# Reordering the prologue of a convolution-and-attention kernel on one core

## The chip, the core and the metric

The kernel runs on one core of one Trainium2 chip. The metric is the device time of one execution in microseconds; a comparison uses the median of several runs. The core has five engines that run side by side and meet through semaphores: TensorE (PE in the profile; its weight loads are PEld), VectorE (DVE), ScalarE (ACT), GpSimd (POOL) and SyncE (SP), whose queue issues every DMA of this kernel. Each engine takes its instructions strictly in the order in which the program gives them.

## The reference

Eight images of 128 channels and 36x36 pixels go through two layers. What matters of them:

```python
# layer 0, on the group-normalised image; residual added outside
x = conv1x1(gn(x), w_x) + b_x
q = conv3x3(x, w_qx, 'SAME');  k = conv3x3(x, w_kx, 'VALID');  v = conv3x3(x, w_vx, 'VALID')
a_x = softmax(q^T k) v
h = tanh(conv1x1(concat([x, a_x], 1), w_h) + b_h)
out = conv1x1(h, w_o) + b_o

# layer 1, on the 1296 tokens of 128 channels of each image
t = tanh(q[:, :, None, :] + k[:, None, :, :])          # additive attention
attn = softmax(einsum('bijd,d->bij', t, w) + bw)
t = t_in + attn @ ln(t_in)
t = t + moe(ln(t))       # 64 experts, each takes its 8 best tokens of an image
```

The input also has a context image `c0` (one value for each channel). It enters `h` only through a constant vector: since a softmax sums to one, the attention over a constant context is its value convolution. The kernel computes that vector once.

## The kernel before

All arrays are float32. The kernel has a prologue for the first image, a long score loop over all images, and an end for the experts.

**The score loop.** The additive attention is written with products of features: for the queries and the keys of a token the kernel keeps exponentials of eight blocks of 128 projected features, and a score is a sum of quotients of matrix products. `units` lists (image, chunk of 432 queries, tile of 128 keys), 8 x 3 x 11 in all, and `slots` cuts a unit into 12 slots (2 for the short last key tile). In each slot `numerators` and, three slots ahead (`LAG`), `denominators` issue small matrix products (L875). ScalarE takes a logarithm and an exponential to invert the denominators (L898, L901), and VectorE and GpSimd multiply and sum (`terms`, L923 to L938). The key features of a tile (`kf`, 512 KB) come from HBM: `keys` computes them (L645, L649), stores them to `kd` (L660), and `prefetch` (L858) loads them two units ahead.

**Work for the next image** is written as generators: `normal` (group normalisation, the 1x1 convolution and the windows for the 3x3 ones), `conv_keys`, `layer0`, `tokens`, `keys`. In the loop four lanes take one piece of a generator at a time between slots, by fixed rules; for the first image the prologue runs the generators through one after another (`drain`). The order of instructions on each engine is thus fixed when the program is built.

**The prologue**, in the order in which it is issued:

- L165 to L179: loads of x of the first image, `w_x`, `b_x` and the small constants; GpSimd fills constants meanwhile (L181 to L213).
- L217 to L227: the context vector: `w_vc` is loaded (576 KB), nine small products and one more make `vc` and then `hb`, the bias of layer 0's tanh.
- L1010: x of the second image is loaded.
- `normal(0)` (L318): it begins with `load_taps` for the keys (L323). The 3x3 convolutions use a scheme with four turned taps in place of three, so `load_taps` loads the raw taps (L304 to L306), turns them on VectorE (L308 to L311) and stores the result in HBM (L313), from where later images load it (L300). Then the statistics of x (L327, L330), two products with the group average `gavg`, the reciprocal root on GpSimd (L239), the scaled weights `wxn` on GpSimd (L350), the 1x1 convolution (L360) and its windows on VectorE (L362 to L375).
- `signs` (L495): GpSimd builds a matrix of signs, 128x1024, with a memset and 22 selects (L505); the features of layer 1 need it.
- `conv_keys(0)`, then `features` (L512): two loads, two transpositions, four products with the sign matrix (L528), and a few small products (L538, L550) that make the constants `a_q`, `a_k`, `cs_s`, `fb_s`, `eb_s` of the loop.
- `layer0(0)` (L390): `load_taps` for values and queries, the value convolution in three groups of rows with four parts each (L403), its product with `w_h` (`pvw`, L411), then for each chunk of 432 pixels the query convolution, the attention, and at last the tanh and the output product.
- `tokens(0)`, the keys of three tiles, three query blocks, `prefetch` of two units, and the denominators of the first three slots.

`big` is a pool of eight buffers for images, taps and the like; `chunks` holds smaller ones. `TAKE`, `step` and `matmuls` are what a generator yields to say what it wants next; `bmm` is a matmul that is counted for the loop's balance, and the profile puts it on L258 (transpositions: L262).

Of the kernel before, what the change touches and what calls it, by code (L numbers as in the profile page):

```python
# [2 lines left out]

# [66 lines left out]
def kernel(  # L70
# [55 lines left out]
    with ExitStack() as loop, ExitStack() as score:  # L126
# [37 lines left out]

        load_x(0)  # L165
        wx_s = loaded(w_x, "w_x")
        bx_s = loaded(b_x, "b_x")
        wh_s = loaded(w_h, "w_h")
# [4 lines left out]
        gw_s = loaded(gate_w, "gate_w")  # L173
        gb_s = loaded(gate_b, "gate_b")
# [4 lines left out]
        nc.sync.dma_start(bw_s, bw.to_broadcast([128, 1]))  # L179
        neg_half = const.tile([128, NT], F32, tag="neg_half", name="neg_half")  # L180
# [33 lines left out]

        wvc_s = big_tile("wvc_s")[:, : 9 * C]  # L217
        nc.sync.dma_start(wvc_s, w_vc.rearrange("i t o -> i (t o)"))
        pv = aux("pv")
        for t in range(9):  # L220
            mm(pv[:, :1], wvc_s[:, t * C : (t + 1) * C], c0_s, start=(t == 0), stop=(t == 8))
        vc = small.tile([C, 1], F32, tag="vc", name="vc")
        nc.vector.tensor_copy(vc, pv[:, :1])
        ph = aux("ph")
        mm(ph[:, :1], wh_s[:, 2, :], vc, start=True, stop=True)
        hb = const.tile([C, 1], F32, tag="hb", name="hb")
        nc.vector.tensor_add(hb, ph[:, :1], bh_s)  # L227
# [65 lines left out]
        turned_taps = {}  # L293

        def load_taps(w, name):

            t = big_tile(name)[:, : 12 * C]
            h = t.rearrange("p (y j c) -> p y j c", y=3, j=4)
            if name in turned_taps:
                nc.sync.dma_start(t, turned_taps[name])  # L300
                return h
            g = w.rearrange("i (y x) o -> i y x o", x=3)
            g1 = chunk_tile("g1")[:, : 3 * C].rearrange("p (y c) -> p y c", y=3)
            nc.sync.dma_start(h[:, :, 0, :], g[:, :, 0, :])  # L304
            nc.sync.dma_start(h[:, :, 3, :], g[:, :, 2, :])
            nc.sync.dma_start(g1, g[:, :, 1, :])  # L306
            half = chunk_tile("half")[:, : 3 * C].rearrange("p (y c) -> p y c", y=3)
            nc.vector.tensor_add(half, h[:, :, 0, :], h[:, :, 3, :])  # L308
            nc.vector.tensor_scalar(half, half, 0.5, None, ALU.mult)
            nc.vector.scalar_tensor_tensor(h[:, :, 1, :], g1, 0.5, half, ALU.mult, ALU.add)  # L310
            nc.vector.scalar_tensor_tensor(h[:, :, 2, :], g1, -0.5, half, ALU.mult, ALU.add)  # L311
            turned_taps[name] = dram.tile([C, 12 * C], F32, tag=name, name=f"{name}_d")
            nc.sync.dma_start(turned_taps[name], t)  # L313
            return h
# [3 lines left out]
        def normal(b):  # L318
# [4 lines left out]
            taps["k"] = load_taps(w_k, "wk_t")  # L323
# [20 lines left out]
            ve = plus_eps(pv[:, :1], 1e-5, [C, 1])  # L344
            yield step(2)
# [37 lines left out]
        def conv_keys(b):  # L383
            k = convolved["k"] = big_tile("k0")
            for r0, nr in KROWS:
                yield from conv_turns(
                    taps["k"], (r0, nr), 1, grid(k[:, r0 * WV : (r0 + nr) * WV], WV), True
                )

        def layer0(b):  # L390
# [5 lines left out]
            wv_t = load_taps(w_v, "wv_t")  # L396
            v = big_tile("v0")
            wq_t = load_taps(w_q, "wq_t")
# [112 lines left out]

        def features(sign):  # L512
# [4 lines left out]
            feat = []  # L517
            for name, wt in (("a_q", wq1), ("a_k", wk1)):
                wt_s = chunk_tile("w_in")[:, :C]
                nc.sync.dma_start(wt_s, wt)  # L520
# [501 lines left out]
        for u in range(2):  # L1022
            prefetch(u)
        for p in range(LAG):
            denominators(p)
# [221 lines left out]
```

## Time and profile before

| | us |
|---|---|
| median of 3 runs | 6183.36 (6181.84 to 6194.64) |
| profiled execution, its own time | 6189.61 |
| its span in the profile | 6187.9 |
| TensorE, ScalarE, VectorE, GpSimd busy | 5946.4, 5275.0, 4799.7, 4584.2 |

Milestones of the profiled execution, from the timeline:

| start, us | what |
|---|---|
| 0.81 | x is issued |
| 12.30 | first product of the context |
| 19.17 | statistics of x |
| 23.09 | `ve`, the variance with epsilon |
| 27.00 | first row of the window buffer (`xpad`) |
| 36.05 to 45.15 | results of the key convolution are added up |
| 25.59 to 50.35 | GpSimd's selects for the signs |
| 60.62 | first product of the value convolution |
| 70.39 | it goes on after a wait |
| 80.22 | first `pvw` |
| 152.18 | output product of layer 0 |
| 172.17 | first keys |
| 183.58 | first denominators of the loop |

The page gives the busy time of each engine, the span in slices, the chain that ended last and the costliest groups of instructions. The timeline lists instructions in order of time with start and duration; the waits list says who waited for whom, the time in total, the count and the longest. In the table of stretches each row has the stretch, its length, the busy time of TensorE, its weight loads, VectorE, ScalarE and GpSimd with counts, then the clock that TensorE was granted (1.00 is full), the busy share of the DMA engines and the GB/s they moved. A matmul in float32 shows as two records.

### The profile page before, as it was taken

How to read it: one execution, taken by the hardware profiler on the slowest of the kernel's cores; microseconds unless marked ns; L12 is line 12 of the kernel's file. 1: busy time of each engine (PE TensorE's matmuls, PEld its weight loads, DVE VectorE, ACT ScalarE, POOL GpSimd, SP SyncE). 2: the span in 40 equal slices, each digit the busy share in tenths (PEclk: the TensorE clock that was granted, in tenths of full speed). 3: DMA queues.
4: the chain of work that ended last, by engine and by line, in shares of the span. 5: the costliest groups of instructions: out<-in, count | busy, mean ns of one | idle time of the engine just before them, and what ended most of it. 6: DMA issues, size and time to landing. Idle time of an engine off the chain costs nothing.

```text
span 6187.9 us, 93159 instructions
## 1 busy us (share of the span) xinstructions
PE 5946.4 (96%) x33576; PEld 2834.5 (46%) x33576; DVE 4799.7 (78%) x9525; ACT 5275.0 (85%) x5371; POOL 4584.2 (74%) x2794
## 2 busy tenths in 40 slices
PE   7999999999999999999999999999999999999996
PEld 5454444544544445444445444454444444544443
DVE  3687778877788787877887777887778878788872
ACT  1798998988989888889988899898998988999980
POOL 3677877777778777778777786877777777787870
PEclk9999999999999999999999999999999999999997
DMA  1210011000110002100111001110011000100017
GB/s 43 70 36 22 21 68 38 33 26 28 67 39 24 26 30 69 37 24 23 50 48 38 22 24 63 41 36 22 21 65 41 31 25 28 63 31 28 25 55 276
DMA packets 150383, 271.40 MB, mean 44 GB/s; under 512 B 45408, under 2 KB 74976, under 8 KB 149920
## 3 DMA queue, kind: packets, MB, share of 16 engines
q1 hardware_dynamic: 149920, 265.44, 12.8%
q8 instruction: 265, 4.34, 0.3%
q14 instruction: 198, 1.62, 0.1%
HBM read 200.94 MB, written 64.19 MB: 43 GB/s over the span
## 4 chain that ended last, share of the span: by engine, by line
PE 65%; DVE 11%; POOL 8%; ACT 8%; issue 8%; DMA 1%; SPq 0%; POOLq 0%; DVEq 0%; ACTq 0%
PE n L875 30%; PE d L875 10%; PE pa L258 7%; ACT lq L898 5%; PE pc L258 5%; DVE n L923 4%; POOL accp L938 4%; DVE rp L929 3%; PE s L258 3%; PE pk L258 3%; DVE accd L925 2%; POOL qf L673 1%; POOL accp L936 1%; PE d L880 1%; PE pq L258 1%
## 5 line engine op out<-in xcount | busy, mean ns | idle before, releaser
L938 POOL TENSOR_TENSOR accp<-accp,rp 128x864 f32<-128x864 f32 x1440 | 2915.1, 2024 | 996.5 <-DVE rp L929 943.5
L875 PE MATMUL n<-qf,kf 32*128 32x432 f32 (+1 forms) x11520 | 3283.6, 574 | 58.9 <-DVE accd L925 19.1
L898 ACT ACTIVATE lq<-d 128x864 f32<-128x864 f32 x2928 | 2517.6, 879 | 555.8 <-PE d L875 498.0
L875 PE MATMUL d<-qf,kf 32*128 32x432 f32 (+1 forms) x11520 | 2907.7, 563 | 46.4 <-ACT lq L898 40.5
L929 DVE TENSOR_TENSOR rp<-n,lq 128x432 f32<-128x432 f32 x3912 | 2160.8, 600 | 557.9 <-PE d L875 398.8
L901 ACT ACTIVATE lq<-lq 128x1728 f32<-128x1728 f32 (+1 forms) x1464 | 2398.2, 1638 | 46.3
L875 PEld LDWEIGHTS n<-qf,kf 32*128 32x128 f32 (+1 forms) x11520 | 1185.9, 185 | 1588.2 <-DVE rp L929 469.1
L875 PEld LDWEIGHTS d<-qf,kf 32*128 32x128 f32 (+1 forms) x11520 | 1046.9, 186 | 449.8 <-issue 241.7
L923 DVE TENSOR_TENSOR n<-n,lq 128x432 f32<-128x432 f32 x1440 | 812.0, 608 | 251.8 <-PE n L875 195.2
L925 DVE TENSOR_TENSOR accd<-n,accd 128x432 f32<-128x432 f32 x1440 | 868.1, 603 | 24.7
L936 POOL TENSOR_TENSOR accp<-rp 128x864 f32<-128x864 f32 x240 | 485.2, 2022 | 244.8 <-DVE rp L929 244.7
L673 POOL TENSOR_SCALAR qf<-qf,cs_s 128x432 f32<-128x432 f32 x192 | 260.7, 1364 | 47.0 <-ACT qf L672 47.0
L258 PEld LDWEIGHTS pa<-xh,e 128*108 128x108 f32 x1920 | 222.1, 174 | 142.9 <-DVE rp L929 63.3
L947 POOL TENSOR_TENSOR accd<-accp,accd 128x432 f32<-128x432 f32 x240 | 265.3, 1106 | 23.3 <-DVE accd L925 3.0
L258 PE MATMUL pa<-xh,e 128*108 128x129 f32 x1920 | 261.3, 283 | 19.9 <-DVE accd L925 13.9
L945 POOL TENSOR_TENSOR accp<-accp 128x432 f32<-128x432 f32 x240 | 264.7, 1103 | 15.8
L258 PE MATMUL s<-q,k 128*116 128x432 f32 x480 | 230.3, 568 | 4.2 <-DVE accd L925 2.7
L444 ACT ACTIVATE e<-s 116x432 f32<-116x432 f32 x240 | 124.8, 520 | 118.7 <-PE s L258 118.4
L258 PEld LDWEIGHTS pk<-xT,a_k 128*128 128x128 f32 x1408 | 171.6, 193 | 105.9 <-DVE n L923 31.8
L435 POOL TENSOR_TENSOR tot<-tot,e 116x432 f32<-116x432 f32 x192 | 212.1, 1105 | 7.3 <-ACT e L444 4.5
L918 DVE TENSOR_TENSOR accd<-n,lq 128x432 f32<-128x432 f32 x240 | 145.1, 604 | 86.7 <-PE n L875 49.7
L258 PE MATMUL pa<-e,vw 116*128 116x432 f32 x480 | 204.6, 549 | 0.0
(208 smaller groups left out, 3870.2 us busy)
## 6 DMA issues: line engine op xcount, KB each, us to landing
kf<-kd SPq DMA_DIRECT2D x240, 512.0 KB
kd<-ks SPq DMA_DIRECT2D x160, 256.0 KB
w<-in_weight_dram SPq DMA_DIRECT2D x32, 1024.0 KB
wk_t<-wk_t_d SPq DMA_DIRECT2D x7, 768.0 KB
wv_t<-wv_t_d SPq DMA_DIRECT2D x7, 768.0 KB
wq_t<-wq_t_d SPq DMA_DIRECT2D x7, 768.0 KB
x<-in_x_dram SPq DMA_DIRECT2D x8, 648.0 KB
t<-tokd SPq DMA_DIRECT2D x96, 54.0 KB
```

The lines of the kernel that those rows point to most:

```text
L258: mm(out, lhsT, rhs, **kw)
L673: nc.gpsimd.tensor_scalar(qf[:, 1, :], qf[:, 0, :], cs_s[:, q : q + 1], None, ALU.mult)
L875: mm(outs[h][:, :CH], kf[rows[h], q, :], qf_of[b, c, q][rows[h], part, :], start=True, stop=True)
L898: nc.scalar.activation(lq[:, o : o + n, :], d[:, :n, :CH], AF.Ln)
L901: nc.scalar.activation(some, some, AF.Exp, scale=-1.0)
L923: mult(ns[h], ns[h], lq[:, o + h, :])
L925: nc.vector.tensor_add(live["d"], ns[h], live["d"])
L929: mult(rp[:, h, :], n, lq[:, o + h, :])
L936: nc.gpsimd.tensor_add(live["p"], live["r"], rp)
L938: nc.gpsimd.tensor_add(live["p"], live["p"], rp)
L945: nc.gpsimd.tensor_add(s[:, 0, :], s[:, 0, :], s[:, 1, :])
L947: nc.gpsimd.tensor_add(d, s[:, 0, :], d)
```

## The change

- The raw taps of keys, values and queries are loaded at the start, right behind x, `w_x` and `b_x`, together with the two inputs of `features`; the other constants follow. x of the second image is loaded when its `normal` begins.
- Turning the taps is a function of its own, `turn_taps`, with an engine as argument and five operations instead of four. For the keys it runs on VectorE, in `normal(0)` behind `ve`; for values and queries on GpSimd, between `normal(0)` and `signs`.
- The context vector and `features` become generators, chained. From the tenth piece of `layer0(0)` on, one of their pieces is issued after each of its pieces; what is left follows behind.
- Only one tile of keys is made before the first query blocks and denominators. Its exponentials go to a `kf` buffer directly and are stored from there; no `prefetch` of unit 0 is made. The next two tiles and the `prefetch` of unit 1 follow behind the denominators.

```diff
+        def load_raw_taps(w, name):
+            h = big_tile(name)[:, : 12 * C].rearrange("p (y j c) -> p y j c", y=3, j=4)
+            g = w.rearrange("i (y x) o -> i y x o", x=3)
+            g1 = chunk_tile("g1")[:, : 3 * C].rearrange("p (y c) -> p y c", y=3)
+            nc.sync.dma_start(h[:, :, 0, :], g[:, :, 0, :])
+            nc.sync.dma_start(h[:, :, 3, :], g[:, :, 2, :])
+            nc.sync.dma_start(g1, g[:, :, 1, :])
+            raw_taps[name] = (h, g1)
+
         load_x(0)
         wx_s = loaded(w_x, "w_x")
         bx_s = loaded(b_x, "b_x")
+        load_raw_taps(w_k, "wk_t")
+        w_in = [loaded(w, "w_in", chunks, "chunk") for w in (wq1, wk1)]
+        load_raw_taps(w_v, "wv_t")
+        load_raw_taps(w_q, "wq_t")
         wh_s = loaded(w_h, "w_h")
...
-        wvc_s = big_tile("wvc_s")[:, : 9 * C]
-        nc.sync.dma_start(wvc_s, w_vc.rearrange("i t o -> i (t o)"))
...
+        def context():
+            wvc_s = big_tile("wvc_s")[:, : 9 * C]
+            nc.sync.dma_start(wvc_s, w_vc.rearrange("i t o -> i (t o)"))
+            yield
+            pv = aux("pv")
+            for t in range(9):
+                mm(pv[:, :1], wvc_s[:, t * C : (t + 1) * C], c0_s, start=(t == 0), stop=(t == 8))
+            yield
...
+        def turn_taps(name, eng):
+            h, g1 = raw_taps[name]
+            half = chunk_tile("half")[:, : 3 * C].rearrange("p (y c) -> p y c", y=3)
+            eng.tensor_add(half, h[:, :, 0, :], h[:, :, 3, :])
+            eng.tensor_scalar(half, half, 0.5, None, ALU.mult)
+            eng.tensor_scalar(g1, g1, 0.5, None, ALU.mult)
+            eng.tensor_add(h[:, :, 1, :], half, g1)
+            eng.tensor_sub(h[:, :, 2, :], half, g1)
+            turned_taps[name] = dram.tile([C, 12 * C], F32, tag=name, name=f"{name}_d")
+            nc.sync.dma_start(turned_taps[name], h.rearrange("p y j c -> p (y j c)"))
...
-            nc.vector.tensor_scalar(half, half, 0.5, None, ALU.mult)
-            nc.vector.scalar_tensor_tensor(h[:, :, 1, :], g1, 0.5, half, ALU.mult, ALU.add)
-            nc.vector.scalar_tensor_tensor(h[:, :, 2, :], g1, -0.5, half, ALU.mult, ALU.add)
...
             ve = plus_eps(pv[:, :1], 1e-5, [C, 1])
+            if b == 0:
+                turn_taps("wk_t", nc.vector)
             yield step(2)
...
         def features(sign):
-            for name, wt in (("a_q", wq1), ("a_k", wk1)):
-                wt_s = chunk_tile("w_in")[:, :C]
-                nc.sync.dma_start(wt_s, wt)
+            for name, wt_s in zip(("a_q", "a_k"), w_in):
                 tp = aux("w_t")
                 nc.tensor.transpose(tp[:, :C], wt_s, ident)
+                yield
...
+                first = (b, t) == (0, order[0])
+                if first:
+                    kf_of[0] = kfp.tile([128, NF, 128], F32, tag="kf", name="kf")
...
-                    ks = kstp.tile([128, NF // 2, 128], F32, tag="ks", name="ks")
+                    if first:
+                        ks = kf_of[0][:, some, :]
+                    else:
+                        ks = kstp.tile([128, NF // 2, 128], F32, tag="ks", name="ks")
...
-        load_x(1)
         drain(normal(0))
+        for name in ("wv_t", "wq_t"):
+            turn_taps(name, nc.gpsimd)
         sign = signs()
         drain(conv_keys(0))
-        a_q, a_k, cs_s, fb_s, eb_s = features(sign)
-        drain(layer0(0), tokens(0), keys(0, order[:3]))
+        aside = chain(context(), features(sign))
+        for i, _ in enumerate(layer0(0)):
+            if i > 8:
+                next(aside, None)
+        drain(aside)
+        a_q, a_k, cs_s, fb_s, eb_s = (feat[n] for n in ("a_q", "a_k", "cs_s", "fb_s", "eb_s"))
+        drain(tokens(0), keys(0, order[:1]))
         for i, q in enumerate(IN_TURN):
...
-        urgent.append(keys(0, order[3:]))
-        for u in range(2):
-            prefetch(u)
         for p in range(LAG):
             denominators(p)
+        drain(keys(0, order[1:3]))
+        prefetch(1)
+        urgent.append(keys(0, order[3:]))
```

## The prediction

> **What bounds the kernel now.** I read the page first, then the waits of TensorE and the timeline of the first 190 us, because the change touches nothing behind them.
>
> ```profile
> span 6187.9 us, 93159 instructions
> ...
> PE 5946.4 (96%) x33576; PEld 2834.5 (46%) x33576; DVE 4799.7 (78%) x9525; ACT 5275.0 (85%) x5371; POOL 4584.2 (74%) x2794
> ...
> PE   7999999999999999999999999999999999999996
> ```
>
> TensorE is busy 96% of the span; only its first and last slices of 155 us fall short. The instruction order of the score loop, past its opening, is the same in both kernels on every engine. So a microsecond saved ahead of the loop moves the whole loop and should reach the end, and the question is what sets the pace of the prologue. TensorE's waits in the first 190 us, with total, count and longest:
>
> ```profile
> PE pv L221 <- DMA wvc_s<-in_w_vc_dram: 12.3, 1, 12.3
> PE pm L258 <- DVE gn_mv L330: 4.1, 1, 4.1
> PE d L875 <- DMA kf<-kd: 4.0, 1, 4.0
> PE pa L528 <- POOL sign L505: 3.8, 1, 3.8
> PE pc L258 <- DVE v L286: 3.4, 1, 3.4
> ```
>
> First `wvc_s`, fifteenth on the load queue; then the statistics; the keys' way through HBM; the sign matrix from GpSimd; and the value convolution's evacuation, which sits on VectorE behind the turning of the query taps.
>
> ```profile
> 19.17 1.62 DVE L327 BATCH_NORM_STATS2 gn_st<-x 128x6 f32<-128x432 f32 x3
> ...
> 28.01 1.82 DVE L372 TENSOR_TENSOR xwin<-xpad 128x216 f32<-128x216 f32 x1
> 29.75 0.37 DVE L374 TENSOR_TENSOR xwin<-xpad 128x216 f32<-128x216 f32 x1
> ...
> 27.76 2.40 POOL L505 TENSOR_SCALAR_AFFINE_SELECT sign<-sign 128x256 f32<-128x256 f32 x1
> ```
>
> (Start, duration.) The statistics start at 19.17 us although x, the first load, needs far less: SyncE's ninth issue waits for the first DMA to end and goes out at 4.69 us. And one subtraction takes 1.82 us where its twin takes 0.37, under a GpSimd select that runs from 27.76.
>
> **The change, step by step.** Times are those of the profiled execution (6189.6 us, span 6187.9); the median of the runs shown is 6183.4, so I take the saving off that median.
>
> *Statistics first.* VectorE no longer has the context's `vc` and `hb` (waiting on `wvc_s`) or the key taps' turning ahead of L327. x is in SBUF at about 4.7 us, so the statistics start 14.5 us earlier, and `ve` comes at 8.6 instead of 23.1 us. The key taps (576 KB behind x) are there by then: the rows around 10 to 14 us move 350 GB/s, which gives 2 us for them; estimate 7 us.
>
> *Key taps on VectorE behind `ve`.* Five operations replace four: 0.56, 0.36, 0.36, 0.56, 0.56 us, 2.4 in all. They are covered: in the trace VectorE idles 2.04 us before `bxn` and 1.55 before the first `xpad`. What is not covered is GpSimd's `rsqrt` (0.57) and `wxn` (0.61), which now start just as these do. The row for two such operations meeting is the 1.82 us above. The Trainium skill (SBUF — State Buffer, "SBUF: two separate sides") states the rule behind it: the read and write ports that VectorE and GpSimd share are an exclusive lock, held for a whole instruction, also against a VectorE operation with two SBUF inputs. By that rule, if VectorE keeps the lock through all five, `wxn` is 2.4 us late; by the row, where selects and subtractions take turns, it waits for the one or two operations in front, about 0.8 us. Ends 0 and 2.4; I take 0.8, since each of the five waits for its predecessor's result and leaves a gap. So the normalisation and the key convolution move up 14.5 - 0.8 = 13.7 us: keys are convolved at 31.5 instead of 45.2 us. Selects lengthened VectorE's `xwin` block by some 3.4 us before (four rows of 1.82, 1.20, 0.98 and 0.76 us against 0.37); turns of about 1 us do so now; no difference taken.
>
> *Value and query taps turned on GpSimd*, twice three two-input operations and two by a scalar, 128x384, ahead of the sign matrix:
>
> ```profile
> L938 POOL TENSOR_TENSOR accp<-accp,rp 128x864 f32<-128x864 f32 x1440 | 2915.1, 2024 | 996.5 <-DVE rp L929 943.5 <-DVE sums L705 1.9 <-DVE pa L707 1.5
> L947 POOL TENSOR_TENSOR accd<-accp,accd 128x432 f32<-128x432 f32 x240 | 265.3, 1106 | 23.3 <-DVE accd L925 3.0 <-DVE ve L234 1.7 <-ACT lq L898 0.6
> L673 POOL TENSOR_SCALAR qf<-qf,cs_s 128x432 f32<-128x432 f32 x192 | 260.7, 1364 | 47.0 <-ACT qf L672 47.0
> L350 POOL TENSOR_SCALAR wxn<-w_x,gn_rs 128x128 f32<-128x128 f32 x8 | 4.9, 610 | 0.8
> L1094 POOL COPY pooled_s<-pooled 128x448 f32<-128x448 f32 x1 | 0.6, 561 | 0.1
> ```
>
> (Busy us, mean ns.) Two inputs: 2.1 ns per column between 432 and 864, so 1.00 us at 384. By a scalar: 2.5 ns per column between 128 and 432, so 1.25 us. A turn is 3 x 1.00 + 2 x 1.25 = 5.5 us, the two 11.0. The skill's GPSIMD Engine Reference ("4.1 Engine selection") calls one-input work roughly line-rate, which the copy row (0.48 at 384) looks like: then the two turns are 2 x (3.0 + 0.96) = 7.9 us. The scalar rows are the same operation, so I take 11.0, plus 1.0 for meeting VectorE, with 7.9 and 16 as ends (16: every one of the ten also waits half a microsecond for the lock).
>
> *The sign matrix* therefore starts later relative to everything else: `wxn` ends at 24.6 - 14.5 + 0.8 = 10.9 us, turns to 22.9, memset and selects take 1.0 + 24.8 us as in the trace, and the matrix is whole at 48.7 us instead of 50.4. This is what is late next: of 13.7 us won, GpSimd gives back all but 1.7.
>
> *Context and features among the value convolution's turns.* Its twelve groups take 1.12 us (216 columns) or 1.0 (198) at full clock. From 31.5: five groups to 37.0; context 18 halves at 0.12 (the row of `pcs`: 16 in 1.95), 2.2 us; groups six to eight with `ph` and a transposition 3.5 us, to 42.7; the first feature product 1.0, to 43.7 (its half of the signs is there). The second waits for the whole matrix until 48.7: 5.0 us, instead of 3.8. Behind it in TensorE's queue stand four groups (4.0), a transposition (0.3), two products (2.0), `pcs` (1.95) and `psw` (0.4). A wait like this costs clock as well:
>
> ```profile
> 48.00:50.00 2.00, 0.00 (x0) 0.00 (x0) 0.00 (x0) 0.00 (x0) 1.86 (x5) 1.00 0.00 0
> 54.00:56.00 2.00, 2.00 (x4) 0.68 (x2) 0.69 (x1) 0.00 (x0) 0.00 (x0) 0.50 0.00 0
> 184.00:186.00 2.00, 1.18 (x8) 0.00 (x0) 0.00 (x0) 0.81 (x2) 0.00 (x0) 0.50 0.27 109
> 186.00:188.00 2.00, 1.87 (x8) 0.64 (x8) 0.00 (x0) 1.97 (x3) 0.00 (x0) 0.50 0.00 0
> ```
>
> (After the five busy times comes the granted clock: after each idle stretch of about 3 us or more in this prologue it is 0.50 for 3 to 7 us.) I charge 2.0 us for 4 us at half speed, and 0.5 for hand-overs between engines. The product of 48.7 ends at 49.8; 49.8 + 8.65 + 2.0 + 0.5 = 60.9 us for the first `pvw`, against 80.2. Gain so far 19.3: 13.7 from the start, 5.6 from here. The 3.4 us stall on the query taps is gone, since they are turned at 22.9 and first used after 60.
>
> *Loads and stores on SyncE.* `wvc_s` now stands behind the stores of the three turned taps, the last of which waits for GpSimd until 22.9: with two 768 KB stores near 300 GB/s it lands at about 29, 8 us before use. x of the second image goes out only with that image's first step; in the trace that slot issues at 256.5, and VectorE reads x at 259.9. 648 KB at 300 GB/s are 2.2 us, behind a 256 KB store: it lands within a microsecond of its use either way, and VectorE's products of the loop stand behind it. Cost 0 to 1.5, taken 0.
>
> *First keys straight to their buffer.* In the trace:
>
> ```profile
> 172.17 0.60 ACT L649 ACTIVATE ks<-pk 128x512 f32<-128x512 f32 x1 [18.75 <-PE pk L258]
> ...
> 177.46 0.60 ACT L649 ACTIVATE ks<-pk 128x512 f32<-128x512 f32 x1 [0.26 <-PE pk L258]
> ...
> 183.58 1.60 PE L875 MATMUL d<-qf,kf 32*128 32x432 f32 x8 [4.03 <-DMA kf<-kd]
> ```
>
> On the old scale: the first tile's second half is exponentiated at 174.4, three query products take 2.3 us behind it, and the first `d` runs at 176.0 instead of 183.6. But the other two tiles now come between the third `d` and the first `n`: four groups of 0.93 us on TensorE and four exponentials of 0.60 on ScalarE, which has two logarithms, an exponential and a third logarithm ahead (to 181.2) and ends them at 183.6. The fourth logarithm follows, where it started at 188.44: 4.8 us; the fifth 5.2 us earlier. I take 5.2. The half-speed rows 184 to 190 should vanish with the 4 us wait.
>
> Sum: 19.3 + 5.2 = 24.5 us, so 6183.4 - 24.5 = 6159 us.
>
> **The rivals.** *(B) GpSimd is quick enough.* With 7.9 us and no meeting cost the signs are whole at 44.6, the wait shrinks to 1 us and the clock stays up: 43.7 + 1 + 1.1 + 8.65 + 0.5 is about 55, gain 25 + 5 = 30, so 6153 us. For it: the copy row. Against: the scalar rows.
>
> *(C) The shared ports bind.* With 16 us of turns and `wxn` 2.4 us late the matrix comes 5.6 us later and all of that is in the sum: gain 19, or 16 if the clock takes two microseconds more; 6164 to 6167 us.
>
> *(D) The loop gives it back.* If the loop's first units waited for something absolute in time, such as the stores of the keys, up to half would go: 6171 to 6181, which can count as no change. Against: between 200 and 6000 us the list of waits has no wait of TensorE or VectorE on a DMA.
>
> *(E) Slower.* x of the second image lands late, and VectorE, in order, holds the loop's products behind L327. It costs one for one from the instant the load misses 259.9, cancels the gain at 24.5 us late and is slower by over 0.2% from 37 us late. With 2.2 us of transfer and no other large load in front that is remote: 6200 us.
>
> **How the numbers follow.** Likeliest (A) 0.52, with its own range 6154 to 6164; B 0.20; C 0.16; D 0.08; E 0.04. 0.2%, about what a measurement of this kernel can tell, is 12.4 us. A, B and C are faster by more; D is split between same and just faster. Faster 0.89, same 0.07, slower 0.04. The range runs from B's end with 4 us for the scatter of the runs, 6149, to C's, 6168.
>
> **What would show it.** The statistics at 4 to 5 us; ten GpSimd rows of 1.0 and 1.25 us ahead of the memset of `sign`; `wxn` near 11; the last select near 49 and a wait of TensorE on it of about 5 us with the clock at half behind; the first `pvw` near 61; the first `d` near 157 with no wait on a DMA; the fourth logarithm near 164. The prediction is wrong if GpSimd's rows are far from these, if `wvc_s` lands after TensorE asks for it, if VectorE waits on x near 235, or if the loop from its twelfth slot on takes longer than before.

## The result and the profile after

The changed kernel takes 6163.30 us (median of 6 runs, 6151.91 to 6166.63) against 6190.86 us of the kernel before in the same set (6 runs, 6181.84 to 6194.64): a ratio of 0.995, 95% interval 0.994 to 0.996. In a later set of runs the same pair came at 6158.15 and 6190.51 us, 0.9946 (0.9934 to 0.9959). So it is faster, by 27.6 and 32.4 us, or 0.5%; the forecast was a saving of 24.5 us, and 6163.30 lies within its range of 6149 to 6168 us. The profiled execution took 6163.47 us with a span of 6161.8, 26.1 less than before.

The head of the page of the changed kernel, busy time first:

```profile
span 6161.8 us, 93158 instructions
...
PE 5932.4 (96%) x33576; PEld 2828.1 (46%) x33576; DVE 4796.5 (78%) x9518; ACT 5274.3 (86%) x5371; POOL 4595.3 (75%) x2804
```

GpSimd is busy 11.1 us longer, about the ten operations added (11.8 us by the timeline); VectorE and ScalarE hardly change. TensorE has the same number of instructions and is busy 14.0 us less, so part of the gain is the clock at which it runs. The stretch up to GpSimd's first closing addition of a unit of the loop ("first sum" below) shows how much; stretch, length, busy with count, clock, busy share of the DMA engines, GB/s, for the kernel before:

```profile
0.00:215.00 215.00, 164.55 (x673) 0.92 0.16 52
```

and for the changed kernel:

```profile
0.00:186.60 186.60, 153.37 (x677) 0.95 0.17 55
```

Of 28.4 us less, 17.2 are idle time of TensorE (50.4 to 33.2 us) and 11.2 are about the same products in less time, at a mean clock of 0.95 instead of 0.92. Adding up, in rows of 0.5 us, TensorE's busy time times what its clock lacks gives 14.3 us lost before and 6.2 after; so the clock column accounts for about 8 of the 11.2. Another 1.9 are the context's 18 records, which took 4.00 us before (from 12.30) and 2.06 now, although the column reads 1.00 at both places; it doesn't show what slowed them. The changed kernel's waits of TensorE in the first 190 us (total, count, longest):

```profile
PE tpn L285 <- DVE xh L640: 7.4, 1, 7.4
PE pm L281 <- DVE gn_mv L350: 6.8, 1, 6.8
PE pa L553 <- POOL sign L529: 5.7, 1, 5.7
PE po L281 <- ACT hpre L506: 2.8, 1, 2.8
```

The waits for `wvc_s` (12.3 us), for the keys through HBM (4.0) and for the value convolution's evacuation (3.4) are gone from the head of this list. The wait for the signs is there and has grown from 3.8 to 5.7. The wait for the statistics now runs from zero to 6.8 us: the load of x to 4.77, then the statistics. The first line, on `xh` behind the attention, stood at 7.1 us before; the change doesn't touch it.

The timeline of the changed kernel, start and duration, TensorE, VectorE and GpSimd in turn:

```profile
10.98 3.89 PE L281 MATMUL px<-x,wxn 128*128 128x432 f32 x6
...
35.27 2.06 PE L242 MATMUL pv<-c,wvc_s 128*128 128x1 f32 x18
...
40.67 1.10 PE L553 MATMUL pa<-sign,wT 128*128 128x512 f32 x2
47.43 2.08 PE L553 MATMUL pa<-sign,wT 128*128 128x512 f32 x2 [5.66 <-POOL sign L529]
...
58.40 2.42 PE L281 MATMUL pvw<-w_h,v 128*116 128x128 f32 x20
...
4.77 1.63 DVE L347 BATCH_NORM_STATS2 gn_st<-x 128x6 f32<-128x432 f32 x3 [2.72 <-DMA x<-in_x_dram]
...
8.70 0.16 DVE L257 TENSOR_SCALAR ve<-pgv 128x1 f32<-128x1 f32 x1 [0.68 <-PE pgv L281]
...
10.04 0.61 DVE L323 TENSOR_TENSOR wk_t<-half,g 128x384 f32<-128x384 f32 x1
10.57 1.35 DVE L324 TENSOR_TENSOR wk_t<-half,g 128x384 f32<-128x384 f32 x1
...
12.87 0.67 DVE L384 TENSOR_SCALAR xpad<-px,bxn 128x432 f32<-128x432 f32 x1 [0.88 <-PE px L281]
...
21.33 0.35 DVE L309 COPY k<-pc 128x204 f32<-128x204 f32 x1
...
10.46 1.05 POOL L320 TENSOR_TENSOR half<-wv_t 128x384 f32<-128x384 f32 x1
11.60 1.35 POOL L321 TENSOR_SCALAR half<-half 128x384 f32<-128x384 f32 x1
...
23.23 24.15 POOL L529 TENSOR_SCALAR_AFFINE_SELECT sign<-sign 128x256 f32<-128x256 f32 x22
```

The statistics start when x has landed, and the two engines that were said to set the pace do so in the order that was said: GpSimd goes from `wxn` into the taps, from the taps (22.26) into the signs (47.38), and TensorE stands before the second feature product until then. The line L324 on VectorE shows what a meeting of the two engines costs: the subtraction that takes 0.55 us where GpSimd is idle (a later run below) takes 1.35 while GpSimd runs its first turning operations.

ScalarE of the changed kernel, where the loop opens:

```profile
154.69 1.67 ACT L933 ACTIVATE lq<-d 128x864 f32<-128x864 f32 x2 [0.31 <-PE d L910]
...
158.71 1.56 ACT L684 ACTIVATE ks<-pk 128x512 f32<-128x512 f32 x3
161.44 0.60 ACT L684 ACTIVATE ks<-pk 128x512 f32<-128x512 f32 x1 [1.17 <-PE d L910]
161.94 0.89 ACT L933 ACTIVATE lq<-d 128x864 f32<-128x864 f32 x1
```

The first logarithm waits for TensorE and no longer for a load. The four exponentials of the next two key tiles stand ahead of the fourth logarithm, as the diff has it.

Milestones beside the forecast, us. The first sum (128x432, L945 before, L980 after) marks how far the loop has been moved.

| | before | forecast | after |
|---|---|---|---|
| statistics start | 19.17 | 4.7 | 4.77 |
| `wxn` ends | 24.6 | 10.9 | 10.48 |
| keys convolved | 45.2 | 31.5 | 30.4 |
| signs whole | 50.4 | 48.7 | 47.4 |
| first `pvw` | 80.22 | 60.9 | 58.40 |
| first `d` | 183.58 | 157 | 153.65 |
| fourth logarithm | 188.44 | 164 | 161.94 |
| first sum | 214.58 | | 186.17 |
| span | 6187.9 | | 6161.8 |

Of the 28.4 us at the first sum, 21.8 were won by the first `pvw` and 6.6 behind it; 26.1 reach the end. The time from the first to the last sum was 5803.7 us before and 5805.9 after, and a second profile of the same changed kernel had 5799.2, so the 2.2 us are no loss that can be told from scatter. In that second profile the first sum came at 184.74, so one profile places it to within about 1.5 us.

### The profile page after: what moved, and what is told of

Read it like the earlier page. It is cut to its first block, busy times and chain, and to the rows that moved or that the text cites. A ratio compares the mean times of both kernels' runs of the same rounds, so it can differ in the third digit from the quotient of the medians.

```text
span 6161.8 us, 93158 instructions
## 1 busy us (share of the span) xinstructions
PE 5932.4 (96%) x33576; PEld 2828.1 (46%) x33576; DVE 4796.5 (78%) x9518; ACT 5274.3 (86%) x5371; POOL 4595.3 (75%) x2804
## 4 chain that ended last, share of the span: by engine, by line
PE 65%; DVE 10%; POOL 8%; ACT 8%; issue 7%; DMA 1%; SPq 0%; POOLq 0%; DVEq 0%; ACTq 0%
PE n L910 30%; PE d L910 10%; PE pa L281 7%; ACT lq L933 6%; PE pc L281 5%; POOL accp L973 4%; DVE n L958 4%; PE s L281 3%; DVE rp L964 3%; PE pk L281 2%; DVE accd L960 2%; POOL qf L708 1%; POOL accp L971 1%; PE d L915 1%; PE pq L281 1%
## 5 line engine op out<-in xcount | busy, mean ns | idle before, releaser
L980 POOL TENSOR_TENSOR accp<-accp 128x432 f32<-128x432 f32 x240 | 264.6, 1103 | 15.8
```

Of the source, the lines that this page charges most:

```text
L980: nc.gpsimd.tensor_add(s[:, 0, :], s[:, 0, :], s[:, 1, :])
```

## The experiments

My theory: the prologue is a chain from x over the statistics and GpSimd (`wxn`, ten turning operations, signs) to the second feature product, and in its tail from the first keys over ScalarE to the fourth logarithm; all that is saved on it reaches the end. The rivals: the gain comes from some part alone (the statistics, the order of features, the keys); GpSimd's taps cost nothing because TensorE would wait for another thing anyway, or could as well run on VectorE; the loop gives back what the prologue wins. Each run below is the changed kernel with the edit shown. The first four ran beside a kernel before of 6189.97 us (16 runs), the next four beside 6191.04 (33 runs), the last three beside 6190.51 (9 runs). Where a median is set against the changed kernel's 6163.30, it is across sets, and two kernels that ran in two sets show how far that reaches: 6163.30 and 6158.15 us for the changed kernel, 6155.03 and 6147.80 for the one with the query taps last. Differences of less than about 7 us between such medians say little; the milestones in the profiles say more.

### The first keys through HBM again

```diff
-                first = (b, t) == (0, order[0])
+                first = False
...
-        drain(tokens(0), keys(0, order[:1]))
+        drain(tokens(0), keys(0, order[:3]))
...
+        urgent.append(keys(0, order[3:]))
+        for u in range(2):
+            prefetch(u)
         pending = deque()
```

(The lines for the next two tiles and for unit 1 behind the denominators are taken out in turn.)

> The changed kernel with its last part undone: three tiles of keys first, all stored to HBM, and both first units fetched from there. My theory (the HBM trip stood on the path): from the first key product to the first denominators 13.5 us again, as in the kernel before (170.1 to 183.6), where the changed kernel has 5.1 (148.6 to 153.7); the fourth logarithm of the loop at about 167 instead of 161.9; 5 us more in all. Rival (the loop takes up the delay, since the same key work is only moved): under 1 us in the end. Everything up to 148 us unchanged in both.

Measured 6173.79 us (6165.49 to 6179.05), ratio 0.997 (0.996 to 0.998). TensorE of this run, timeline:

```profile
150.10 7.45 PE L281 MATMUL pk<-xT,a_k 128*128 128x128 f32 x48
...
163.50 1.19 PE L910 MATMUL d<-qf,kf 32*128 32x432 f32 x8 [3.76 <-DMA kf<-kd]
165.63 1.81 PE L910 MATMUL d<-qf,kf 64*128 64x432 f32 x4 [0.95 <-ACT lq L933]
```

From the first `pk` to the first `d` it is 13.4 us here and 5.1 in the changed kernel; the wait on the load of `kf` is back, and the products behind it run at half clock (1.81 us for four against 0.99). From the first `pk` to the first sum it is 44.4 us against 37.6: this part is worth 6.8 us. (The first sum itself is 8.3 us later; 1.5 of it lies ahead of the first `pk`, where the edit changes nothing.) The median is 10.5 us above the changed kernel's; in this profile the end behind the last sum was also 7 us longer (177.1 against 169.7), and nothing that the edit touches lies there.

### Query taps turned last

```diff
-        for name in ("wv_t", "wq_t"):
-            turn_taps(name, nc.gpsimd)
+        turn_taps("wv_t", nc.gpsimd)
+        side = context()
+        next(side)
         sign = signs()
+        turn_taps("wq_t", nc.gpsimd)
...
-        aside = chain(context(), features(sign))
+        aside = chain(side, features(sign))
...
-            if i > 8:
+            if i > 9:
```

The load of `wvc_s` is issued ahead of the signs, so that it doesn't stand behind the store of the query taps.

> GpSimd turns the value taps, makes the signs, and only then turns the query taps; the load of the context's weights is issued before the store of the query taps, so that it does not stand behind them on SyncE. My theory (after the change the signs are what TensorE waits for, since 11.8 us of turning stand ahead of them): the last select ends near 41.5 instead of 47.4, TensorE's wait of 5.7 us falls to under 0.5 and its clock is not halved behind it; first pvw at about 52 instead of 58.4; 6.5 us less in all, about 6157 where the changed kernel has 6163. Rival (the wait moves on): the query taps, turned at about 47.5, or the context's weights are then late, and under 2 us are won.

Measured 6155.03 us (6139.96 to 6160.88), ratio 0.9941 (0.9929 to 0.9954). GpSimd and TensorE of this run:

```profile
17.71 24.32 POOL L529 TENSOR_SCALAR_AFFINE_SELECT sign<-sign 128x256 f32<-128x256 f32 x22
42.00 1.00 POOL L320 TENSOR_TENSOR half<-wq_t 128x384 f32<-128x384 f32 x1
...
42.84 1.88 PE L553 MATMUL pa<-sign,wT 128*128 128x512 f32 x4
```

The signs are whole at 42.0 and all four halves run without a wait. The first `pvw` comes at 52.56 instead of 58.40, the first sum at 180.52 instead of 186.17: 5.7 us, of which the time shows 8.3. So GpSimd's order was what bound the changed kernel here, and a query tap ahead of the signs costs about a microsecond for each microsecond of its turning.

### The same, with the context's load behind the query taps' store

```diff
-        for name in ("wv_t", "wq_t"):
-            turn_taps(name, nc.gpsimd)
+        turn_taps("wv_t", nc.gpsimd)
         sign = signs()
+        turn_taps("wq_t", nc.gpsimd)
```

> As e3_query_taps_last, but the load of the context's weights stays behind the store of the turned query taps on SyncE's queue. My theory (SyncE issues in order, so the load waits for a GpSimd operation at 47 us): the load goes out at about 47.7 and lands near 52; TensorE, which wants it at 35.3, waits 17 us; first pvw near 70 instead of 58.4, 10 to 13 us more than the changed kernel in all. Rival (the load finds its way past a waiting store): as e3_query_taps_last, 6.5 us less.

Measured 6172.44 us (6168.58 to 6184.17), ratio 0.9973 (0.9963 to 0.9984). SyncE's queue in this run, then TensorE's wait:

```profile
47.20 0.32 SPq L326 DMA_DIRECT2D wq_t_d<-wq_t  x1
47.57 0.43 SPq L238 DMA_DIRECT2D wvc_s<-in_w_vc_dram  x1
```

```profile
PE pv L242 <- DMA wvc_s<-in_w_vc_dram: 17.0, 1, 17.0
```

The store waits for GpSimd and the load stands behind it; the first `pvw` falls to 71.47 and the first sum to 197.85, 11.7 us after the changed kernel's. The same edit of GpSimd's order is worth minus 5.7 or plus 11.7 us by the place of one DMA in a queue.

### The taps turned on VectorE, and a second form of it

```diff
         for name in ("wv_t", "wq_t"):
-            turn_taps(name, nc.gpsimd)
+            turn_taps(name, nc.vector)
```

> The changed kernel with the value and query taps turned on VectorE at the same place in the program, so behind the windows of the key convolution, 10 operations of 0.36 to 0.56 us, 4.8 us in all. Theory (what counts is how late the signs are): the signs are whole near 36 us, TensorE does not wait for them, but the key convolution's evacuations start 4.8 us later, so that it ends near 35; 11.9 us of work to the first feature products and 9.7 behind: first pvw near 56.7 instead of 58.4, 1 to 2 us less in all. Rival (GpSimd relieves VectorE, which sets the pace): 4.8 us more.

Measured 6167.62 us (6165.72 to 6169.59), ratio 0.9964 (0.995 to 0.9978), first `pvw` at 62.76, first sum at 190.60: 4.4 us later than the changed kernel, where earlier was expected. The rival's 4.8 us is near this, but it counted operations at their undisturbed 4.8 us, which is not what the run shows. VectorE of this run:

```profile
13.92 1.82 DVE L394 TENSOR_TENSOR xwin<-xpad 128x216 f32<-128x216 f32 x1
...
24.50 1.83 DVE L323 TENSOR_TENSOR wv_t<-half,g 128x384 f32<-128x384 f32 x1
...
26.73 1.94 DVE L320 TENSOR_TENSOR half<-wq_t 128x384 f32<-128x384 f32 x1
```

The selects start at 11.51 here and run beside VectorE. The ten turning operations take 10.2 us (21.96 to 32.17) where their uncontended durations sum to 4.8, and the windows ahead of them 9.0 us; TensorE waits 10.7 us for the first copy of the key convolution behind them. To see whether it is the meeting with the selects and not VectorE, the selects were kept off by giving VectorE the memset of `sign`, in its order behind the taps:

```diff
-            nc.gpsimd.memset(sign, 0.0)
+            nc.vector.memset(sign, 0.0)
...
-            turn_taps(name, nc.gpsimd)
+            turn_taps(name, nc.vector)
```

> As e8_turned_on_vectore, but the memset of the sign matrix is VectorE's, behind the turned taps, so that GpSimd runs no select before that; only the time of VectorE's block from the first window row to the last turned tap is of interest. Theory (GpSimd's selects lock the shared SBUF port against VectorE's operations with two SBUF inputs and its fast scalar ones): the windows take 5.6 us instead of 9.0 and the ten turning operations 4.8 us instead of 10.1, the block 10.5 instead of 19.2; the signs, 24 us of selects behind it, are whole near 49, so the total is no better. Rival (these operations are slow by themselves at this place): block as in e8_turned_on_vectore, 19 us.

One run, 6164.19 us. VectorE and GpSimd:

```profile
18.75 0.55 DVE L320 TENSOR_TENSOR half<-wv_t 128x384 f32<-128x384 f32 x1
...
22.67 0.55 DVE L324 TENSOR_TENSOR wq_t<-half,g 128x384 f32<-128x384 f32 x1
...
24.37 24.15 POOL L529 TENSOR_SCALAR_AFFINE_SELECT sign<-sign 128x256 f32<-128x256 f32 x22 [13.65 <-DVE sign L522]
```

The same ten operations take 4.5 us (18.75 to 23.22), the windows 5.7. So the meeting with the selects is the cause of the doubling. It gains nothing over the changed kernel (first sum 188.03): the signs are whole at 48.5 instead of 47.4, since the taps on VectorE come behind the windows, and GpSimd idles for 13.65 us.

### The context first, and the features ahead of layer 0

Two parts of the new order undone one by one. First the context vector at its old place, ahead of the statistics:

```diff
+        drain(context())
...
-        aside = chain(context(), features(sign))
+        aside = features(sign)
```

> The changed kernel with the context vector computed ahead of the first normalisation again: its load is the twenty-sixth on SyncE, and its nine products, vc and hb stand ahead of the statistics on TensorE and VectorE. My theory (a late start passes whole, because GpSimd's turning and signs hang on the normalisation): the load lands near 17.5, the products take 4 us at half clock, the statistics start near 22 instead of 4.8; every later milestone up to the first denominators 17 us later, first pvw near 76, about 17 us more in all. Rival (the signs bind, so the start of the statistics has slack): under 6 us more.

Measured 6182.0 us (6174.98 to 6189.22), ratio 0.9987 (0.998 to 0.9993). Waits of VectorE, first 30 us:

```profile
DVE vc L245 <- PE pv L242: 20.6, 1, 20.6
```

VectorE stands before `vc` for 20.6 us with x long in place; the statistics start at 23.60, 18.8 us late, and the first sum comes at 207.14, 21.0 late. 18.8 of it is the start. The wait for the signs is 10.1 us, because without the context among its groups TensorE reaches the features with six groups of the convolution still behind them, and not four.

Then the features and the context run through ahead of layer 0:

```diff
-        for i, _ in enumerate(layer0(0)):
-            if i > 8:
-                next(aside, None)
-        drain(aside)
+        drain(aside, layer0(0))
```

> The changed kernel with context and features run through between the key convolution and layer 0, as before, instead of between the turns of the value convolution. My theory: TensorE ends the keys at 30.4, waits for the signs until 47.4 with only the first half of the features to do, then runs the rest one after another for 10 us (50.4 to 60.6 in the kernel before); the value convolution starts near 57.5 and takes 12.5 to 14 us: first pvw near 71 instead of 58.4, 13 us more in all. Rival (TensorE waits for the signs either way, so the interleaving brings nothing): under 3 us.

Measured 6181.35 us (6173.85 to 6187.73), ratio 0.9985 (0.9977 to 0.9994), first `pvw` at 73.86, first sum at 200.60, 14.4 us late. TensorE's waits in the first 80 us of this run:

```profile
PE pa L553 <- POOL sign L529: 12.3, 2, 10.2
```

With nothing else to do, TensorE waits 12.3 us for the signs instead of 5.7. The groups of the value convolution are the cover for the signs; without them half of the change's gain goes (14.4 of 28.4 us at the first sum).

The parts undone one at a time cost 21.0, 14.4 and 6.8 us at the first sum, together more than the 28.4 gained: they lean on each other, and none is a share of the gain. The early loads of the taps and the place of the key taps behind `ve` were not undone alone.

### The second image's x ahead of its use

The query taps last, as above, and one line more, ahead of `tokens(0)`:

```diff
+        load_x(1)
         drain(tokens(0), keys(0, order[:1]))
```

> As e3_query_taps_last, with x of the second image loaded at the end of layer 0 of the first image. Theory: VectorE's wait of 1.0 us on that load at 225 us disappears and the loop is 1 us earlier from there, 6154 us where e3_query_taps_last has 6155; nothing else moves. Rival: the wait has slack behind it, and nothing is won; or the load is in the way of the stores of the first tokens near 131 us, and up to 2 us are lost.

Measured 6158.68 us (6151.57 to 6171.52), ratio 0.9948 (0.9936 to 0.9961); by time this can't be told from the run without that line (0.9941). In the changed kernel VectorE waits for this load once, by its timeline:

```profile
232.41 0.61 DVE L347 BATCH_NORM_STATS2 gn_st<-x 128x6 f32<-128x432 f32 x1 [1.24 <-DMA x<-in_x_dram]
```

With the early load that wait is gone, which confirms its cause; whether its microsecond reaches the end stays open.

### The small products spread, and two kernels a second time

In the run with the query taps last the granted clock fell to 0.50 twice while TensorE was busy throughout, each time behind a run of very small products (18 of one column, 16 of two). Was it these? The following edit spreads them over the convolution's turns, with the two edits above in place:

```diff
             for t in range(9):
                 mm(pv[:, :1], wvc_s[:, t * C : (t + 1) * C], c0_s, start=(t == 0), stop=(t == 8))
-            yield
+                if t % 2 == 0:
+                    yield
...
-            yield
+                if q % 2 == 1:
+                    yield
```

> The query taps turned last and the second image's loads ahead of the first image's tokens (both as in the run of the second image early), and beside that the 18 products of one column and the 16 of two columns no longer in one run each but in groups between the convolution's turns. Theory S (a run of tiny products lets the clock fall by half although TensorE is busy, as the clock of 0.50 behind each of the two runs suggests): no half clock between 34 and 60 us here, first product of vw at 51 us or before, sum over the first unit at 178 to 179.5 us, 1 us ahead of the run with the query taps last alone. Theory R (the fall has another cause, since the run of the second image early had the same order on TensorE and kept a clock of 1.00): the half clock comes or stays away whatever the order, sum over the first unit at 179 to 181 us. Both expect a time within 3 us of the run with the query taps last, 7 to 10 us below the changed kernel.

> The kernel with the query taps turned last, looked at a second time beside the two others of this set. Theory S: the clock falls to 0.50 again at 39 to 42 us and at 53 to 56 us, behind the tiny products. Theory R: it may stay at 1.00 in one or both places, and the sum over the first unit then comes at 179 to 180 us instead of 180.5. Either way a ratio to the kernel before of 0.993 to 0.995, and 5 to 8 us below the changed kernel of this set.

> The changed kernel unaltered, so that it and the two others share the runs of the kernel before. TensorE waits for the signs 5 to 6 us, the clock is at half for some 5 us behind that wait (both theories: here an idle stretch comes before it), sum over the first unit at 186.2 us, ratio to the kernel before 0.994 to 0.996.

Measured: spread 6156.96 us (6155.06 to 6160.07), ratio 0.9944 (0.9931 to 0.9956); query taps last again 6147.80 (6143.45 to 6151.41), 0.9929 (0.9915 to 0.9943); the changed kernel again 6158.15 (6152.86 to 6167.08), 0.9946 (0.9934 to 0.9959). The stretches of TensorE (stretch, length, busy with count, granted clock, busy share of the DMA engines, GB/s), first in the first run with the query taps last:

```profile
38.00:40.00 2.00, 2.00 (x11) 0.76 0.00 0
40.00:42.00 2.00, 2.00 (x8) 0.50 0.00 0
42.00:44.00 2.00, 2.00 (x8) 0.89 0.00 0
...
52.00:54.00 2.00, 2.00 (x13) 0.67 0.04 8
54.00:56.00 2.00, 2.00 (x12) 0.50 0.00 0
56.00:58.00 2.00, 2.00 (x14) 0.98 0.00 0
```

then in the second run of the same kernel:

```profile
38.00:40.00 2.00, 2.00 (x14) 1.00 0.00 0
40.00:42.00 2.00, 2.00 (x11) 1.00 0.00 0
...
54.00:56.00 2.00, 2.00 (x13) 1.00 0.00 0
```

and with the small products spread:

```profile
52.00:54.00 2.00, 2.00 (x14) 0.71 0.27 107
54.00:56.00 2.00, 2.00 (x6) 0.50 0.00 0
56.00:58.00 2.00, 2.00 (x11) 0.94 0.00 0
```

The half clock is absent from the one with the order that was to bring it, and present in the one with the order that was to prevent it. So Theory S as it was put, the same order and so the same clock, falls. The small products as a cause do not fall with it, for the traces hold more. Taking the clock as either full or half, a row of 2 us with a mean clock c has 4 x (1 - c) us at half, so each of the three stretches above is 3.4 us long: 39.0 to 42.4, 52.7 to 56.1, and 52.8 to 56.2 in the last run. The other half-clock stretches of these prologues are 3.4 us or a multiple, such as 6.8 (44.7 to 51.5 in the changed kernel) and 10.2 (25.4 to 35.6 with the taps on VectorE), and within a run their starts lie multiples of 3.4 apart (52.68 - 39.03 = 4 x 3.41). So the clock seems to be set by intervals of 3.4 us, whose borders fall differently in each run.

In the first run each set of small products (18 and 2 of one column, from 35.80 to 38.95; 16 of two columns and 2 of one, from 49.55 to 52.56) lies whole in the interval ahead of a half-clock stretch. In the second, with the borders reckoned back from its half clock at 122.5, one cuts each set: at 37.2 within the 18, at 50.8 ahead of the last two at 51.02. And the kernel that was to spread them kept the 16 within 49.95 to 52.60, inside one interval, 49.4 to 52.8, right ahead of its half clock; its 18, cut by a border at 39.2, had none behind them. This account was found afterwards, and no run tests it by itself. It is not complete either: the spread kernel's last two came behind the interval (53.41) and the clock fell, while in the changed kernel the 16 lay in one interval (54.9 to 58.3), the last two across its end, and it stayed.

What a stretch costs: in the second run the first `pvw` came at 51.16 instead of 52.56. Yet its first sum at 181.09 was no earlier, because it had more half clock later (122.5 to 129.3 and 132.7 to 146.4 us, against 134.6 to 144.8 in the first run), on the transpositions and the first `pk` (3.78 us for 16 halves against 2.94).

Two more expectations missed. The spread kernel was to be within 3 us of the one with the query taps last; in their common set it is 9.2 us slower, its fastest run (6155.06) above the other's slowest (6151.41), with the first sum at the same place (180.71 and 181.09). Which of its two further edits costs this, and where, stays open. And the changed kernel's half clock behind the wait for the signs was 3.4 us long in its second profile (47.1 to 50.5), where some 5 were expected.

The last two runs show which of these two kernels is better. With the query taps last it was 8.3 us below the changed kernel by the medians of different sets, and 10.4 us below it in a common one, where the slowest of its five runs (6151.41) is under the fastest of the other five (6152.86). The first sums differ by 5.7 and 3.7 us in the profiles; 5796.4 and 5799.2 us from first to last sum are another 2.8; the rest of the 10.4 is not located, as the spread kernel's 9.2 is not. That version, one tap's turning moved behind the signs with the context's load kept ahead, is the best found here.

## Why the prediction was right, step by step

*A microsecond ahead of the loop reaches the end.* Right: 28.4 us at the first sum, 26.1 at the end. The runs that shift the start agree: 5.7, 11.7 and 4.4 us at the first sum stood as 8.3, 9.1 and 4.3 in the medians. With the context first (21.0 and 18.7) and the features ahead (14.4 and 18.1) it holds to within 4 us. That is as close as medians from different sets can show it, and closer than one could count on. The rival in which the loop gives half of it back is ruled out at this size.

*Statistics first.* Right, 4.77 against 4.7, and the run with the context first shows that without it three quarters of the gain are lost (21.0 of 28.4 us at the first sum).

*Key taps on VectorE.* The price of 0.8 us for meeting GpSimd's two small operations was too high for the path: from the start of `ve` to the end of `wxn` it is 1.78 us after and 1.51 before, so 0.3. The meeting turned out the other way: GpSimd got in first, and VectorE's fifth operation took 1.35 us instead of 0.55, covered by 0.88 us of idle before `xpad`. The keys were convolved at 30.4 and not 31.5: 0.4 is this, and 0.6 is the block of windows on VectorE, where the prediction took no difference. From the first `xpad` to the first copy of the key convolution it is 8.46 us beside GpSimd's turning operations (12.87 to 21.33) and was 9.05 beside its selects (27.00 to 36.05). That `px` took 3.89 us in this profile is no part of it: in the second profile it took 4.67, as before, and the block was 8.46 again.

*Ten operations on GpSimd.* Taken 12.0 us from 1.00, 1.25 and a meeting cost, measured 11.8. Two inputs took 1.05 to 1.22 us, a scalar 1.16 to 1.35. The choice of the scalar rows over the copy row was the right one: the Trainium skill's GPSIMD Engine Reference ("4.1 Engine selection") has one-input work at about line rate, which would have been 0.48 us by the copy row and a total of 7.9; here the one-input multiplication by a scalar was as slow as two-input work. Rival B rested on it and falls with it. Rival C, 16 us, falls too.

*Signs late next.* Right: whole at 47.38 (48.7), TensorE waits 5.66 us (5.0), and the clock is at half behind it. Stretches of the changed kernel (after the busy times, the clock):

```profile
46.00:48.00 2.00, 0.57 (x1) 0.50 (x2) 0.00 (x0) 0.00 (x0) 1.31 (x3) 0.50 0.00 0
48.00:50.00 2.00, 2.00 (x5) 1.04 (x4) 0.46 (x1) 0.00 (x0) 0.00 (x0) 0.50 0.00 0
50.00:52.00 2.00, 2.00 (x9) 1.90 (x8) 0.71 (x3) 0.00 (x0) 0.00 (x0) 0.62 0.00 0
```

TensorE resumes at 47.4, and half speed lasts to 51.5 (the mean of 0.62 in the last row leaves 1.5 us of it at half): 4.1 us, where 4 were charged. That the clock is 0.50 after each idle stretch of about 3 us was read too widely, though: in the profile of before TensorE also stood idle from 17.1 to 21.2, and the rows behind read 1.00 (whether the column is to be trusted that early is another matter, as with the context's products). And in the second profile of the changed kernel only 2.9 us of the half speed fell on work, behind the same wait; so the 4 us were in part luck. What was late next was priced by the run that takes it away: 5.7 us. The first `pvw` is 2.5 us ahead of the forecast: 1.3 because the signs are whole sooner (0.4 of it `wxn`, 0.2 the taps, 0.7 the selects, 25.1 us with the memset against 25.8, which fits VectorE meeting them less), and 1.2 because the work behind them took 11.0 us and not the 12.2 of the sum. Its 2.0 for the clock was right; the parts at full clock came to about 9 and not 10.2, with the feature products, the small products and the 0.5 us for hand-overs each taken too large.

*`wvc_s`.* Right that it was safe, at 35.27 with no wait. How near the edge its place is, the run with the load behind the query taps' store shows.

*x of the second image.* Bounded 0 to 1.5 us, taken at nothing; VectorE waits 1.24 us. The bound held, the value chosen was a microsecond too low or without effect. A wait of VectorE on x near 235 was among the signs of being wrong; it came, at 231 to 232.4 us, and was too small to tell in the time. So did the longer loop, by 2.2 us in one profile and not in the other.

*First keys straight to their buffer.* The mis-sized term: 5.2 us forecast, 6.6 us between first `pvw` and first sum (7.6 in the second profile), 6.8 by the run that undoes it. At the fourth logarithm it is 4.7 (108.2 us from `pvw` before, 103.5 after), as the count of exponentials in front of it said. What the sum left out is the half clock behind the wait on the load: the forecast had those rows vanish but gave them no price. In the run that undoes this part `n` and `d` take 1.09 and 0.93 us until 169 us, where they take 0.53 to 0.63 in the changed kernel.

Together 24.5 us forecast and 28.4 at the first sum: 2.5 from before `pvw`, 1.4 from the tail. The start of the scale moved as well: the median of before was 6183.36 when the forecast was made and 6190.86 over six runs, so an absolute time of 6159 was 4.3 us low while the saving was 3.1 us too small. That these two errors partly cancel in the absolute time is luck; the saving, 24.5 against 27.6 us, is what the forecast can be judged by.

## What to carry to other kernels

When a chain of loads, statistics and set-up tables opens a kernel, write down for each engine and each DMA queue what stands in front of the first thing that the bounding engine needs: here one in-order wait on an unrelated load cost 19 us, and one store in front of one load turned a gain of 6 us into a loss of 12. Of work that is moved to an idle engine ask what on that engine becomes late; the operand needed last goes last, behind the table that is needed first. Before moving two-input work between VectorE and GpSimd, look at what the other one does in those microseconds: side by side, the same ten operations took 10.2 us, apart 4.5.

## What the runs showed of the hardware

The granted clock of TensorE falls to half in stretches of 3.4 us or a multiple, on borders that differ from run to run, and also where no idle stretch comes before: at 39.0 to 42.4 and 52.7 to 56.1 us in one run with 2.00 of 2.00 us busy, at neither place in a second run of the same kernel. In the three runs of the query taps last and the spread products such a fall came only behind an interval of 3.4 us that held all 18 or all 16 of a set of products of one or two columns; it did not follow each such interval. A stretch costs up to half its length (the first `pvw` 52.56 against 51.16), and so a single profile of this prologue is uncertain by 1 to 2 us, whatever the edit.

VectorE and GpSimd side by side do not slow each other evenly: single operations of VectorE took up to 1.9 us instead of 0.55 or 0.37, while their neighbours in the same stretch kept their usual time. The Trainium skill ("SBUF: two separate sides", in SBUF — State Buffer) describes a lock held for a whole instruction. The pair of runs with the selects beside VectorE's taps and behind them agrees with it, at 10.2 against 4.5 us.

That an engine takes its instructions in the order of the program showed twice in the times: VectorE stood before `vc` for 20.6 us with x in place, and SyncE issued the load of `wvc_s` at 47.57 us instead of 22.66, behind a store that waited for GpSimd.
